# Scan layers of a four-layer network on one core: the step size's Softplus and its product with the input move two slots later, and GpSimd's share of B moves to other slots

## The chip, the cores and the metric

The kernel runs on one core of one Trainium2 chip. The core has five engines with their own instruction streams: PE (TensorE, matrix products), DVE (VectorE), ACT (ScalarE), POOL (GpSimd) and SP (SyncE, which here only issues DMA transfers). An engine executes its instructions strictly in the order in which the program lists them; engines wait for each other through semaphores. The metric is the device time in microseconds (us) of one execution.

## The reference

The network works on 8 images of 48 x 48 pixels and 96 channels. Four layers follow one another, each of the form x = x + layer(groupnorm(x)). Layers 0 and 3 are two-dimensional selective scans: a projection to 192 channels and a gate z, a 3 x 3 depthwise convolution with SiLU, four scans over the pixels (rows, columns, and both backwards), a layer norm, the gate and an output projection. Layer 1 is a pointwise network between an up- and a downsampling filter. Layer 2 has four selective scans along rows and columns. What matters here is the scan of layers 0 and 3 (K = 4 directions, 192 channels, 16 states, L = 2304 pixels):

```python
x_dbl = jnp.einsum('bkdl,kcd->bkcl', xs, x_proj_weight)
dts, Bs, Cs = jnp.split(x_dbl, [R, R + N], axis=2)
dts = jnp.einsum('bkrl,kdr->bkdl', dts, dt_projs_weight)
A = -jnp.exp(A_logs.astype(jnp.float32)).reshape(K, Din, N)
delta = jax.nn.softplus(dts + dt_projs_bias.reshape(K, Din)[None, :, :, None])

def step(h, inp):
    u, dl, Bv, Cv = inp
    dA = jnp.exp(dl[..., None] * A)
    h = h * dA + (dl * u)[..., None] * Bv[:, :, None, :]
    y = jnp.einsum('bkdn,bkn->bkd', h, Cv)
    return (h, y)
```

The step size delta is a Softplus; its product with the input u is the second thing that every scan needs. Each of the 192 x 16 pairs of channel and state is a recurrence of its own along the pixels.

## The kernel before

**Blocks, units, slots, turns.** `scans` (from L224) runs a scan layer. The work of one image and one direction is cut into five blocks of pixels (`BLKS`: four of 10 rows, 480 pixels, and one of 8 rows, 384 pixels, called a small block here). Layers 0 and 3 have 8 x 4 x 5 = 160 blocks each. A block has 24 units: a unit is 128 recurrences (32 channels by 4 states) along the block's pixels. Units are grouped in 8 slots of three (`ORDER`: slots 0 to 3 are the first half of the channels, 4 to 7 the second, the four state groups forwards and then backwards, so slots 3 and 4 share their states). Two slots make a turn; a block has four turns, called q0 to q3 here.

**What happens to a unit.** ACT computes dA = exp(A * delta) into PSUM (`make_da`, L329; two units are a pair, three pairs are a turn; the PSUM tile `ps_da` has two buffers, so ACT is at most two pairs ahead). A product du * B is made into the tile `dbu` (`make_dbu`, L305): for some units on DVE, which reads B from a copy in PSUM (`ps_b`, one buffer, written by ACT in `copy_b`, L286), and for the others on POOL, which reads B from the loaded tile `bc`. The tables `ON_POOL_SS` (layers 0 and 3) and `ON_POOL_L2` (layer 2) say how many of a slot's three units POOL makes; where it makes all three, no copy is made. `copy_b` has a case in which slot 4 reuses the copy of slot 3; it needs slot 3 to have one. DVE then runs the recurrence over a pair in place (`scan`, L337). POOL multiplies by C (`make_hc`, L343), and PE sums over the states (`reduce`, L359 to L365) into the tile `ps_y`; ACT copies the finished half block out (`done`, L762).

**The order.** It is written out by hand in the loop at the end of `scans`. For the turn t it lists: scan of pair 0; POOL's multiplication for the second slot of the turn before; DVE's product for slot 2t+2; exponentials of pair 1; POOL's units of slots 2t+2 and 2t+3; scan of pair 1; exponentials of pair 2; the copy of B for slot 2t+3 and DVE's product for it; `aside(2t)`; `begin` (boundary columns two turns ahead, POOL's L314 and L317); POOL's multiplication for the first slot; exponentials of the next turn's pair 0; scan of pair 2; the copy of B for slot 2t+4; `aside(2t+1)`. So products are made one turn before the scan that uses them.

**`aside`, the slot's side work.** Each call first lets ACT read what the guest put into PSUM in the slot before (`guest.settle`); then issues loads on SP (`LOAD_BC`: B and C of the next block at slots 1, 1, 6, 7, L270; `LOAD_DD_SS`: step sizes and products of the next block, in two halves at slots 3 and 5, L258, each 1452 KB when broadcast to 128 partitions); then advances the layer's own side work by one step (`side`: layer norm and output of the image before, group norm and convolution of the image after; the convolution ends in a SiLU group, L595 and L597, in slot 2 of ten of an image's twenty blocks); then runs the preparation steps that are due (`run`); and then lets the guest go on. The guest is layer 1, woven into the scans of layer 0 and layer 2. It matters in layer 0; layer 3 has none.

**Preparation of a block** (`stage1` of `ss2d`, L704 to L748). A block's steps are listed by slot, counted from the start of the second block before it; slots from 8 (`NG`) on lie in the block just before it:

- slot -1 and 1: projection to B, C and the low-rank step size (`s0`, L721, and its copy `s1`, L726)
- slot 3: store of B and C to DRAM (L729) and the first half of the step size's projection (L711)
- slots 4 and 5: the two halves with their bias into the tile `dds`, which has one buffer (`make_room`, `biased`, L715)
- slot 6: `s6`, the Softplus over both halves in one instruction (L739). The profile shows one `ACT_TABLE_LOAD` before it and one before the exponentials after it; the group is called the Softplus burst here
- slot 7: `make_du` (L507 to L515), POOL's product of step size and u, and two small memsets
- slots 8 and 9, that is slots 0 and 1 of the next block: `store_dd`, three stores to DRAM for each half (L492)

After them come the loads of slots 3 and 5 that bring both halves back, broadcast over partitions.

Of the kernel before, what the change touches and what calls it, by code (L numbers as in the profile page):

```python
# [29 lines left out]
NG = 8  # L30
# [14 lines left out]
FAR = 1e30  # L45
CH = 96

ON_POOL_SS = {2: 1, 3: 3, 5: 1, 6: 1, 7: 3}
ON_POOL_L2 = {4: 3, 6: 3, 7: 3}


# [51 lines left out]
def vss_stack_kernel(ctx: ExitStack, tc: tile.TileContext, i: dict, out: bass.AP):  # L103
# [386 lines left out]
    def store_dd(b, half):  # L490
        for g in range(3):
            nc.sync.dma_start(b.dd[half][:, 2 * g * b.m:2 * (g + 1) * b.m],  # L492
                              b.dds[32 * g:32 * g + 32, half].rearrange("p t m -> p (t m)"))

    def sizes(b, half):

        return [b.dds[:, half, n, b.at] for n in range(2)]

    def make_room(b, pools):
        b.room = pools["dds"].tile([DH, LEAD + 4 * WMAX], F32, tag="dds", name="dds")  # L500
        b.dds = b.room[:, LEAD:LEAD + 4 * b.m].rearrange("p (h t m) -> p h t m", h=2, t=2)

    def make_du(b, u):


        dt, du = [b.dds[:, :, n, b.at].rearrange("p h (r s) -> p h r s", s=SEG) for n in range(2)]
        nc.gpsimd.tensor_mul(du, dt, u)  # L507
        if b.m == b.n:
            at = SEG - 1 if b.rev else 0
            nc.gpsimd.memset(dt[:, :, :, at:at + 1], FAR)  # L510
        else:

            far = b.dds[:, :, :, b.came:] if b.back else b.room[:, :4 * b.m].rearrange("p (u m) -> p u m", m=b.m)[:, :, :LEAD + 1]
            nc.gpsimd.memset(b.dds[:, :, :, 0:1] if b.back else b.dds[:, :, :, b.goes:], 0.0)
            nc.gpsimd.memset(far, FAR)  # L515


    def ss2d(l, xin, xout, guest=None):
# [185 lines left out]
        def stage1(b):  # L704
            n = b.n
            u, uall = b.view(us[b.job], dirs[b.k][0]), b.view(uss[b.job], dirs[b.k][0])
            got = {}

            def raw(half):
                got["p"] = ps("s1", 1)  # L710
                nc.tensor.matmul(got["p"][:, :n], lhsT=wide("dtw", (2 * b.k + half) * DH), rhs=b.bcl[:, :n],  # L711
                                 start=True, stop=True)

            def biased(half):
                nc.scalar.activation(sizes(b, half)[0], got["p"][:DH, :n], AF.Identity,  # L715
                                     bias=w[f"{l}_dtb"][:, b.k, half:half + 1])

            def s0():
                got["p"] = ps("s1", 1)
                for half in range(2):  # L720
                    nc.tensor.matmul(got["p"][:, :n], lhsT=wide("xp", (2 * b.k + half) * NBC), rhs=uall[:, half],  # L721
                                     start=(half == 0), stop=(half == 1))

            def s1():
                b.bcl = pools["bcl"]
                nc.scalar.copy(b.bcl[:NBC, :n], got["p"][:NBC, :n])  # L726

            def s3():
                nc.sync.dma_start(b.bcd, b.bcl[:2 * NS, :n])  # L729
                raw(0)  # L730

            def s4():
                make_room(b, pools)
                biased(0)
                raw(1)

            def s6():
                both = b.dds[:, :, 0, b.at]
                nc.scalar.activation(both, both, AF.Softplus)  # L739

            def du():
                make_du(b, u)

            def store(half):
                return lambda: store_dd(b, half)

            return {-1: s0, 1: s1, 3: s3, 4: s4, 5: lambda: biased(1), 6: s6, 7: du,
                    NG: store(0), NG + 1: store(1)}  # L748

        def so_far(b, half):  # L750
            if b.job not in yss:
# [19 lines left out]
        for _ in conv(0, BLKS[:1]):  # L771
            pass
        scans(dirs, (0, 1, 3, 2), False, ON_POOL_SS, a, pools, ps, stage1, opening, done, side, tail, conv(0, BLKS[1:3]), guest)
        for _ in post(nb - 1, BLKS[:1]):
            pass
# [581 lines left out]
```

## Time and profile before

| | us |
|---|---|
| median of 3 executions | 17072.15 |
| their lowest and highest | 17067.16, 17077.52 |
| the profiled execution's own time | 17055.76 |
| its span, first to last instruction | 17054.0 |
| DVE busy | 15779.9 (93%) |
| POOL busy | 15177.8 (89%) |
| ACT busy | 13897.9 (81%) |
| PE busy | 13001.0 (76%) |

The span holds the three scan layers one after another: layer 0 until about 5740 us, layer 2 from about 5830 to 11550 us, layer 3 from about 11650 us on. A line of a group reads: line of the kernel, engine, operation, written tile <- read tiles, shapes, count, then busy us and mean ns of one instruction, and last the engine's idle time just before these instructions with what ended most of it. A line of a timeline reads: start us, duration us, engine, line, operation, tiles and shapes, count of merged instructions, and in brackets the idle time before it and what ended that. Durations in a timeline overlap the next instruction's start by some 0.05 to 0.1 us, so lengths in sums are taken from start to start. A line of stretches reads: from:to, length, then busy us and instruction counts of PE, PEld, DVE, ACT and POOL, the granted PE clock, the DMA engines' busy share and GB/s.

### The profile page before, as it was taken

The page shows a single profiled execution, that of the slowest core. Times are in us where ns is not written, and L with a number is a line of the kernel's source. Part 1 is how long each engine was busy: PE and PEld are TensorE (multiplying, and loading weights), DVE is VectorE, ACT ScalarE, POOL GpSimd, SP SyncE. Part 2 cuts the span into 40 slices and gives each one's busy share as a digit, 9 for nine tenths or more (in the row PEclk, how much of TensorE's full clock was granted, in tenths as well). Part 3 has the DMA queues.
Part 4 walks back from the last instruction along what each step waited for, and adds up shares of the span by engine and source line. Part 5 has one row for each costly group of instructions (what it writes and reads, how often), then busy time and mean ns, then how long its engine had stood idle before and what let it go on. Part 6 is the DMA issues. An engine that isn't in the chain of part 4 may idle for free.

```text
span 17054.0 us, 172343 instructions
## 1 busy us (share of the span) xinstructions
PE 13001.0 (76%) x53740; PEld 4650.8 (27%) x53740; DVE 15779.9 (93%) x9680; ACT 13897.9 (81%) x20972; POOL 15177.8 (89%) x7999
## 2 busy tenths in 40 slices
PE   6778787888787777777777777776777777777776
PEld 1223232333332333233323332221222222222221
DVE  7999999998999799999999999997999999999998
ACT  6888888888787688888888888886877878878876
POOL 7998998998889788888888888887999999999998
PEclk7888888888898899899989998887888878878887
DMA  4555555464555444544454444444555455555554
GB/s 148 180 173 169 180 168 186 166 187 165 175 173 177 137 156 164 163 159 163 157 170 158 158 163 158 161 156 133 176 175 175 175 172 178 176 169 178 176 175 143
DMA packets 931144, 2844.04 MB, mean 167 GB/s; under 512 B 396668, under 2 KB 464988, under 8 KB 803406
## 3 DMA queue, kind: packets, MB, share of 16 engines
q1 hardware_dynamic: 930222, 2833.03, 49.6%
q8 instruction: 422, 6.91, 0.2%
q14 instruction: 500, 4.10, 0.1%
HBM read 2384.40 MB, written 448.17 MB: 166 GB/s over the span
## 4 chain that ended last, share of the span: by engine, by line
POOL 24%; DVE 22%; ACT 21%; issue 18%; PE 10%; DMA 3%; SPq 1%; POOLq 0%; DVEq 0%; ACTq 0%
DVE dbu L337 14%; POOL dbu L343 14%; ACT ps_da L329 8%; POOL dbu L305 6%; DVE dbu L305 6%; ACT L329 3%; POOL dds L507 3%; PE ps_y L363 2%; ACT ps_b L286 2%; DMA dd<-dds 1%; DMA bc<-bcd 1%; PE ps_side L582 1%; ACT L926 1%; PE ps_s L711 1%; ACT zb L926 1%
## 5 line engine op out<-in xcount | busy, mean ns | idle before, releaser
L337 DVE TENSOR_TENSOR_SCAN dbu<-ps_da,dbu 128x968 f32<-128x968 f32 (+3 forms) x5760 | 11825.5, 2075 | 827.6 <-ACT ps_da L329 686.8
L343 POOL TENSOR_TENSOR dbu<-dbu,bc 128x1440 f32<-128x1440 f32 (+1 forms) x3840 | 10062.4, 2633 | 1531.0 <-DVE dbu L337 998.1
L329 ACT ACTIVATE ps_da<-dd,w_l_a 128x484 f32<-128x484 f32 (+3 forms) x11520 | 7420.1, 649 | 2411.1 <-DVE dbu L337 2183.4
L363 PE MATMUL ps_y<-dbu,w_red 128*32 128x480 f32 (+1 forms) x23040 | 4267.1, 656 | 1720.6 <-POOL dbu L343 1658.4
L365 PE MATMUL ps_y<-dbu,w_red 128*32 128x480 f32 (+1 forms) x7680 | 4227.6, 656 | 0.0
L305 DVE TENSOR_TENSOR dbu<-dd,ps_b 128x962 f32<-128x962 f32 (+5 forms) x2720 | 3813.9, 1402 | 185.2 <-ACT ps_b L286 135.2
L305 POOL TENSOR_TENSOR dbu<-dd,bc 128x481 f32<-128x481 f32 (+3 forms) x2080 | 3881.4, 1882 | 0.0
L363 PEld LDWEIGHTS ps_y<-dbu,w_red 128*32 128x32 f32 x23040 | 709.0, 117 | 5153.9 <-POOL dbu L343 3665.4
L286 ACT COPY ps_b<-bc 128x482 f32<-128x482 f32 (+3 forms) x2720 | 1449.0, 533 | 117.7 <-DVE dbu L305 104.2
L582 PE MATMUL ps_side<-xpad,w_l_cw 128*128 128x480 f32 (+1 forms) x2880 | 1324.2, 598 | 46.9 <-ACT g_room L1183 16.6
L329 ACT ACT_TABLE_LOAD x993 | 1274.0, 1283 | 17.5
L711 PE MATMUL ps_s<-bcl,square 128*128 128x480 f32 (+1 forms) x1280 | 876.8, 776 | 233.6 <-ACT dds L715 81.0
L359 PE MATMUL ps_y<-big,eye 128*128 128x480 f32 (+1 forms) x960 | 741.4, 860 | 257.5 <-ACT big L762 253.0
L721 PE MATMUL ps_s<-big,square 128*128 128x480 f32 (+1 forms) x1280 | 848.6, 794 | 66.7 <-ACT g_room L1183 18.3
L507 POOL TENSOR_TENSOR dds<-dds,big 96x960 f32<-96x960 f32 (+1 forms) x320 | 706.2, 2207 | 118.3 <-ACT dds L739 115.6
L582 PEld LDWEIGHTS ps_side<-xpad,w_l_cw 128*128 128x128 f32 x2880 | 560.8, 205 | 792.9 <-issue 675.8
L874 PE MATMUL ps_sb<-xpad,square 128*128 128x480 f32 (+1 forms) x1280 | 608.0, 621 | 89.0 <-ACT g_room L1183 38.0
L365 PEld LDWEIGHTS ps_y<-dbu,w_red 128*32 128x32 f32 x7680 | 647.9, 117 | 0.0
L874 PE MATMUL ps_sa<-xpad,square 128*128 128x480 f32 (+1 forms) x1280 | 521.2, 548 | 0.0
L917 PE MATMUL ps_sa<-xpad,square 128*128 128x480 f32 (+1 forms) x320 | 255.6, 895 | 339.6 <-ACT g_room L1183 108.8
L762 ACT COPY big<-ps_y 96x480 f32<-96x480 f32 (+1 forms) x640 | 471.1, 736 | 38.2 <-PE ps_y L365 36.9
L711 PEld LDWEIGHTS ps_s<-bcl,square 128*128 128x128 f32 x1280 | 250.6, 241 | 762.6 <-ACT dds L715 327.7
(250 smaller groups left out, 12540.6 us busy)
## 6 DMA issues: line engine op xcount, KB each, us to landing
dd<-dd SPq DMA_DIRECT2D x512, 1452.0 KB
bc<-bcd SPq DMA_DIRECT2D x1536, 480.0 KB
dd<-dd SPq DMA_DIRECT2D x256, 1440.0 KB
dd<-dds SPq DMA_DIRECT2D x1536, 121.0 KB
dd<-dd SPq DMA_DIRECT2D x128, 1164.0 KB
bc<-bcd SPq DMA_DIRECT2D x384, 384.0 KB
dd<-dds SPq DMA_DIRECT2D x768, 120.0 KB
dd<-dd SPq DMA_DIRECT2D x64, 1152.0 KB
```

The costliest lines, as they stand in the source:

```text
L286: nc.scalar.copy(bps[t][:, :bcs[t][0].shape[1]], bcs[t][0])
L305: engine.tensor_mul(o, du, by.unsqueeze(1).to_broadcast([P, hi - lo, by.shape[1]]))
L329: nc.scalar.activation(da[:, at:at + b.m], b.got[half][:, u % 3, 0, :], AF.Exp, scale=a[:, b.k, ci:ci + 1])
L337: nc.vector.tensor_tensor_scan(db, da, db, 0.0, ALU.mult, ALU.add)
L343: nc.gpsimd.tensor_mul(h, h, bcs.pop(2 * t + sub)[1].unsqueeze(1).to_broadcast([P, 3, n]))
L363: nc.tensor.matmul(y[32 * g:32 * g + 32, :n], lhsT=wc["red"][:, :32], rhs=hc[:, g, b.at], start=False, stop=(slot == 3))
L365: nc.tensor.matmul(y[DH:, :n], lhsT=wc["red"][:, 32:], rhs=hc[:, 2, b.at], start=False, stop=(slot == 3))
L507: nc.gpsimd.tensor_mul(du, dt, u)
L582: nc.tensor.matmul(pu[:, :n], lhsT=flat[:, at:at + P], rhs=xpad[:, r0 + dy:r0 + dy + nr, dx:dx + W], start=(tap == 0), stop=(tap == 8))
L711: nc.tensor.matmul(got["p"][:, :n], lhsT=wide("dtw", (2 * b.k + half) * DH), rhs=b.bcl[:, :n], start=True, stop=True)
L721: nc.tensor.matmul(got["p"][:, :n], lhsT=wide("xp", (2 * b.k + half) * NBC), rhs=uall[:, half], start=(half == 0), stop=(half == 1))
L874: nc.tensor.matmul(got["u", half][:, :n], lhsT=wide("cw", at), rhs=shifted(off), start=(tap == 0), stop=(tap == 3))
```

## The change

Three edits, for layers 0 and 3 alone; layer 2 is not touched.

- The Softplus moves from slot 6 of the second block before to slot 8, that is from q3 of that block to q0 of the next one (slot 0).
- POOL's product and memsets move from slot 7 to slot 9 (slot 1 of the block before), and all six stores follow them there; before, three stores stood in slot 8 and three in slot 9.
- POOL makes all three units of slot 1 and one of slot 3, where it made one of slot 2 and three of slot 3. Its total stays 9 of 24. Slot 3 now has a copy of B, so `copy_b` lets slot 4 reuse it, and slot 1 has none.

```diff
-ON_POOL_SS = {2: 1, 3: 3, 5: 1, 6: 1, 7: 3}
+ON_POOL_SS = {1: 3, 3: 1, 5: 1, 6: 1, 7: 3}
...
             def du():
                 make_du(b, u)
-
-            def store(half):
-                return lambda: store_dd(b, half)
-
-            return {-1: s0, 1: s1, 3: s3, 4: s4, 5: lambda: biased(1), 6: s6, 7: du,
-                    NG: store(0), NG + 1: store(1)}
+                for half in range(2):
+                    store_dd(b, half)
+
+            return {-1: s0, 1: s1, 3: s3, 4: s4, 5: lambda: biased(1), NG: s6, NG + 1: du}
```

## The prediction

> **What bounds the kernel.** I read the page's busy shares and groups first, then busy time by stretches, then the list of waits, then the timelines of single blocks.
>
> ```profile
> PE 13001.0 (76%) x53740; PEld 4650.8 (27%) x53740; DVE 15779.9 (93%) x9680; ACT 13897.9 (81%) x20972; POOL 15177.8 (89%) x7999
> ...
> L337 DVE TENSOR_TENSOR_SCAN dbu<-ps_da,dbu 128x968 f32<-128x968 f32 (+3 forms) x5760 | 11825.5, 2075 | 827.6 <-ACT ps_da L329 686.8
> ...
> 2000.00:3000.00 1000.00, 810.40 (x3639) 326.59 (x3639) 924.88 (x560) 838.11 (x1302) 897.61 (x510) 0.87 0.56 177
> ...
> 13000.00:14000.00 1000.00, 740.49 (x2868) 224.72 (x2872) 970.01 (x604) 788.54 (x1199) 949.63 (x539) 0.80 0.51 173
> ```
>
> The stretches list PE, PEld, DVE, ACT, POOL. DVE is the bound: layer 0 (60 to 5700 us) leaves it about 75 us idle in 1000, layer 3 (from 11640 us) only 30. Most of that idle time is a scan waiting for its exponentials from ACT: the list of waits has 642 of them, the longest 4.2 us. So only DVE's gaps can move: layer 0 and layer 3 hold some 590 us of them.
>
> A block is four turns, q0 to q3, of two slots. In each, DVE runs scan, product (even slot), scan, product (odd slot), scan. ACT runs one block of layer 3 so (start, duration):
>
> ```profile
> 12742.76 1.28 ACT L595 ACT_TABLE_LOAD   x1
> ...
> 12745.19 1.28 ACT L329 ACT_TABLE_LOAD   x1
> ...
> 12758.91 0.56 ACT L286 COPY ps_b<-bc 128x482 f32<-128x482 f32 x1
> 12759.49 1.28 ACT L739 ACT_TABLE_LOAD   x1
> 12760.78 1.01 ACT L739 ACTIVATE dds<-dds 96x960 f32<-96x960 f32 x1
> 12761.81 1.28 ACT L329 ACT_TABLE_LOAD   x1
> ```
>
> and DVE beside it:
>
> ```profile
> 12740.51 1.63 DVE L305 TENSOR_TENSOR dbu<-dd,ps_b 128x1443 f32<-128x1443 f32 x1
> ...
> 12744.14 1.13 DVE L305 TENSOR_TENSOR dbu<-dd,ps_b 128x962 f32<-128x962 f32 x1
> ...
> 12747.89 2.17 DVE L337 TENSOR_TENSOR_SCAN dbu<-ps_da,dbu 128x968 f32<-128x968 f32 x1 [0.53 <-ACT ps_da L329]
> ...
> 12760.87 1.63 DVE L305 TENSOR_TENSOR dbu<-dd,ps_b 128x1443 f32<-128x1443 f32 x1
> 12762.42 4.26 DVE L337 TENSOR_TENSOR_SCAN dbu<-ps_da,dbu 128x968 f32<-128x968 f32 x2
> ```
>
> Two bursts, two geometries. After the Softplus burst (the three lines from 12759.49) the first exponential starts at 12763.10: 3.61 us. It sits in q3, where DVE has two products of three units (1.55 us each, start to start), and the next scan just does not wait. The Silu burst (12742.76 to the exponential at 12746.49, 3.73 us) sits in q1, with products of three and two units (1.55 and 1.05): there the scan waits 0.53.
>
> **Part 1: the burst goes to q0, and q0 gets q1's geometry.** The units change makes slots 2 and 3 products of three and two units on DVE. With T0 the start of slot 2's product: copy of B ends T0+2.17 (product 1.55, then the copy starts 0.12 late and takes 0.50), burst +3.61, two exponentials and signal 1.45, so T0+7.23. DVE arrives at T0+1.55+2.08+1.05+2.08 = 6.76. Stall 0.47 per full block, close to Silu's 0.53; by the same steps 1.2 in a block of 8 rows (scans 1.69, products 1.25 and 0.85). Going through the DVE and ACT timelines block by block, with the side work that stands at q0 (DVE side work of 0.5 us or more covers the stall; an ACT reading for the guest or a normalization lengthens it): layer 0 has 72 bare full blocks (34 us), 17 with ACT work before the burst (15), 40 covered (0), 31 small (48): 97 us. Layer 3: 93 bare (43), 35 covered (0), 30 small (41): 84 us. Added: 181 us (155 and 205 if a bare block costs 0.41, Silu's wait less the shorter burst, or 0.53).
>
> What goes is the wait of scans 2 to 8.5 us after the burst's first load. Summed over the timeline: 150 us in layer 0, 33 in layer 3. It is large in layer 0 because the guest's products of slot 5 are read by ACT just ahead of the burst. They stay in q3, which DVE now passes faster (no slot 1 product): exponentials must be ready at T0+5.71. Taking each block's measured end of that reading, 25 blocks of layer 0 still wait, 20 us (bounds 0 and 40). Removed: 183-20 = 163. **Net +18 us.**
>
> **Part 2: units.** GpSimd does 9 of 24 units before and after, DVE 15, with the same shapes, so both busy times stay. Slot 4 now reuses slot 3's copy of B: one ACT copy (0.55) less in 319 blocks, 175 us of ACT. I cost it at nothing: it lies in q0 and q3 where ACT waits for DVE anyway; were that not so, it would be worth at most those 175. DVE's turns become 8.8, 8.8, 7.3, 7.8 us instead of 7.3, 8.8, 7.3, 9.4. Hence three small things:
> - Side work of DVE in slot 1 waits for PE. DVE comes there 1.55 later, so each wait shrinks by up to that: 27 us in layer 0, 15 in layer 3: **-42** (bounds -58, all of those waits, and 0, if PE slips as much).
> - Side work in slot 7 (39 operations fed by PE) comes 1.55 earlier, while GpSimd, by the row sums, enters q3 0.9 us less late: 0.65 each, **+25** (bounds 0 and 60).
> - In small blocks a product waits for the boundary copy L317 behind GpSimd's units of slots 2 and 3 (18 us); GpSimd now has one unit there, 1.03 us, not 3.74: **-18** (bounds -18 and +18, should the three units in q3 delay other boundary copies as much).
>
> **Part 3: product and stores to slot 1.** GpSimd: one product (1.88, or 2.70 when columns are read) and memsets of 0.1, moved past two multiplications by C (2.7 each) and slot 3's unit. Summing q0 from its entry 2.1 us late: 2.7+1.0+2.7+2.1 ends 10.6 us after q0's start (11.3 for columns); the next multiplication was due at 9.3, so GpSimd is 1 to 2 us late, and its next consumer, slot 5's unit, has 4 us in hand: 0. On SP, the six stores (0.42 each) now stand behind the two B/C loads of slot 1 and wait for the product:
>
> ```profile
> 12769.21 1.55 SPq L492 DMA_DIRECT2D dd<-dds  x3
> 12770.93 0.52 SPq L258 DMA_DIRECT2D dd<-dd  x1
> ```
>
> Queued behind them are slot 1's and 2's guest transfers, the load L258 of slot 3 and the store of B and C. The first three stores are issued at 12766.66 now, as soon as the product is done. The load issues 6.4 us into q0 and is wanted 26 us into it. Then: product 11, stores 2.8, first landing: 15.5, wanted at 28 (small block 14.8 and 23). By the stretches of 1 us, the traffic of such a load, issued at 13033.2, ends at 13039.5: 6.3 us. So it is hidden, with 6 and 2 us over. The next block's step sizes (L715, slot 4) reuse the buffer, at 21.8 against stores landed by 16.5: 0. At each layer's start slot 1's copy and DVE product (2.28 us, ahead of the first exponential) go: **-5** (bounds -5 and +8, two steps of later stores).
>
> **Sum:** 18-42+25-18-5 = -22 us on the profiled execution's 17055.76 us (span 17054.0): 17034. The median shown is 17072.15, 16.4 above, so **17050 us**, -0.13%. About 0.2%, 34 us, is what tells a change of this kernel from none.
>
> ACT's table loads, by the rows above: an instruction follows a load's end within 0.03 us. The Trainium skill ("ScalarE: Activation LUTs", What ACT_TABLE_LOAD costs) adds a drain of some 1.38 us to each switch; by it a burst would stall every uncovered q0 2.8 us more, about +670 over the 243 turns left uncovered. The trace disagrees, and I go by it.
>
> **Rivals.**
> - *A load comes late (slower).* For it: 2 us of margin in small blocks, two 1452 KB loads back to back, one SP queue. Against: 20 us of margin now, and no scan or product waits for that load after the starts. If both halves land together, 2.9 MB at the 400 GB/s of those stretches, with 1.3 us until bytes flow, takes 8.6 us, past the 8.2 there; each us beyond costs 61 us over the 61 small blocks. It decides from 10 us: two late us are +122 on the sum: 17170. Milder, one: 17110.
> - *Even turns drain other gaps (clearly faster).* In layer 0 scans wait 165 us in the rest of the block, most for exponentials that came late behind guest readings; layer 3 has 73. If the lighter q3 and the missing copy take a third, 80 us: 16970. Against: most of these lie in q1 and q2, which the change leaves as they are.
> - *Only the stall moves.* 181 us come, 183 go, PE-fed waits cancel too: 17070.
>
> **How the numbers follow.** Sum as worked out 0.48 (own range 17010 to 17090, from the bounds of parts 1 and 2, so 0.14 of it is faster by over 0.2%), late load 0.19, drained gaps 0.20, stall only moved 0.13 (of which 0.05 slips to slower by ACT's lateness). Faster 0.34, same 0.42, slower 0.24. The range reaches to the drained gaps and to a load late by one: 16965 to 17120.
>
> **What would show it.** In layer 3's bare blocks, a scan's wait of 0.4 to 0.5 us after each Softplus, at the second turn's start, where now there is none; in layer 0's convolution blocks the wait after Softplus down from 1.3 to about 0.6 us a block; ACT copies of L286 fewer by some 319; DVE and GpSimd busy times unchanged. Wrong if a product L305 waits for dd's load, if SP waits on the product long after slot 3, or if GpSimd's multiplications, not DVE, set layer 3's pace.

## The result, and the profile after

The changed kernel takes 17140.79 us (median of 5, 17132.05 to 17144.43), the kernel before 17067.16 beside it: 1.0043 times as long, 95% interval 1.0032 to 1.0054. The forecast was 17050 us, range 16965 to 17120. It is slower by some 74 us, where a small gain was expected.

The profiled executions differ by 88.6 us. First scan to last scan:

| | before | after | difference | forecast, its terms added by layer |
|---|---|---|---|---|
| layer 0 | 5642.2 | 5729.0 | +86.8 | about -55 |
| layer 2 (not touched) | 5707.9 | 5712.8 | +4.9 | 0 |
| layer 3 | 5363.7 | 5366.1 | +2.4 | about +35 |

So nearly all of the loss lies in layer 0, although layers 0 and 3 got the same edits. (The differences of a few us elsewhere are the size of what two executions differ by: layer 2, which no run edits, takes 5704 to 5714 us in the profiled runs.) The busy shares and the scans' group on the page of the changed kernel, and its stretches (columns as before: PE, PEld, DVE, ACT, POOL):

```profile
PE 12967.6 (76%) x53740; PEld 4655.0 (27%) x53740; DVE 15789.2 (92%) x9680; ACT 13766.5 (80%) x20653; POOL 15193.3 (89%) x7999
...
L337 DVE TENSOR_TENSOR_SCAN dbu<-ps_da,dbu 128x968 f32<-128x968 f32 (+3 forms) x5760 | 11837.3, 2076 | 948.3 <-ACT ps_da L329 790.5
```

```profile
2000.00:3000.00 1000.00, 802.12 (x3526) 318.07 (x3526) 898.60 (x543) 804.29 (x1242) 876.28 (x499) 0.86 0.56 172
13000.00:14000.00 1000.00, 726.05 (x2908) 226.29 (x2912) 973.31 (x597) 780.04 (x1171) 952.97 (x532) 0.83 0.53 177
```

DVE and POOL do the same work; what grew is the scans' wait for exponentials, 686.8 to 790.5 us. The stretch in layer 0 lost 26 us of DVE work in 1000, the one in layer 3 gained 3. ACT did 131 us less, and no gain of it can be seen.

Layer 3 behaves as the prediction drew it. One of its blocks, ACT and then DVE (lines from about L745 on have numbers two lower than before):

```profile
12821.46 0.56 ACT L286 COPY ps_b<-bc 128x482 f32<-128x482 f32 x1 [0.18 <-DVE dbu L305]
12822.04 1.28 ACT L739 ACT_TABLE_LOAD   x1
12823.34 1.01 ACT L739 ACTIVATE dds<-dds 96x960 f32<-96x960 f32 x1
12824.36 1.28 ACT L329 ACT_TABLE_LOAD   x1
12825.66 1.37 ACT L329 ACTIVATE ps_da<-dd,w_l_a 128x484 f32<-128x484 f32 x2
```

```profile
12819.80 1.63 DVE L305 TENSOR_TENSOR dbu<-dd,ps_b 128x1443 f32<-128x1443 f32 x1
...
12823.43 1.13 DVE L305 TENSOR_TENSOR dbu<-dd,ps_b 128x962 f32<-128x962 f32 x1
12824.47 2.17 DVE L337 TENSOR_TENSOR_SCAN dbu<-ps_da,dbu 128x968 f32<-128x968 f32 x1
12827.06 2.17 DVE L337 TENSOR_TENSOR_SCAN dbu<-ps_da,dbu 128x968 f32<-128x968 f32 x1 [0.42 <-ACT ps_da L329]
```

With T0 = 12819.80 the scan starts at T0+7.26 (forecast T0+7.23) and waits 0.42 (forecast 0.47). On SP the stores wait for POOL's product, and the load of the next step sizes goes right behind them:

```profile
12829.33 2.65 SPq L492 DMA_DIRECT2D dd<-dds  x6
12832.30 0.52 SPq L258 DMA_DIRECT2D dd<-dd  x1
```

No scan waits for that load in either layer, and a product only once (2.08 us at 5485.57 us, in layer 0).

Where layer 0's time went is seen by adding up DVE's idle time in its timeline by place in the block (a turn has scans 1 to 3; "product" is L305):

| DVE idle, us | layer 0 before | layer 0 after | layer 3 before | layer 3 after |
|---|---|---|---|---|
| q0, scan 1 (after the burst in slot 6, before) | 148.5 | 9.7 | 33.0 | 0 |
| q0, product of slot 2 | 0 | 16.1 | 0 | 0 |
| q0, scan 2 | 18.6 | 73.5 | under 6 | under 6 |
| q1, scan 1 (after the burst in slot 0, after) | 8.2 | 166.6 | 0 | 76.9 |
| side work in slot 1 that waits for PE | 43.2 | 13.7 | 14.6 | 1.3 |
| q1, product of slot 4 (boundary copy L317) | 5.0 | 0 | 13.1 | 0 |

Two entries were not forecast: the second scan of a block, and how large the burst's stall is in layer 0. Behind both stands the same thing. Here is one and the same block of layer 0 in both kernels, at the same point of layer 1's work. First ACT and DVE of the kernel before:

```profile
3982.50 1.28 ACT L739 ACT_TABLE_LOAD   x1
...
3986.12 1.37 ACT L329 ACTIVATE ps_da<-dd,w_l_a 128x484 f32<-128x484 f32 x2
3987.42 0.54 ACT L286 COPY ps_b<-bc 128x482 f32<-128x482 f32 x1
3988.29 0.40 ACT L1194 COPY g_room<-ps_s 73x288 f32<-73x288 f32 x1 [0.33 <-PE ps_s L1192]
3988.59 2.65 ACT L329 ACTIVATE ps_da<-dd,w_l_a 128x484 f32<-128x484 f32 x4
```

```profile
3987.52 2.17 DVE L337 TENSOR_TENSOR_SCAN dbu<-ps_da,dbu 128x968 f32<-128x968 f32 x1 [2.19 <-ACT ps_da L329]
3989.61 1.13 DVE L305 TENSOR_TENSOR dbu<-dd,ps_b 128x962 f32<-128x962 f32 x1
3990.66 2.17 DVE L337 TENSOR_TENSOR_SCAN dbu<-ps_da,dbu 128x968 f32<-128x968 f32 x1
```

Then the changed kernel, PE first:

```profile
4042.58 0.48 PE L365 MATMUL ps_y<-dbu,w_red 128*32 128x384 f32 x1
4043.00 1.88 PE L582 MATMUL ps_side<-xpad,w_l_cw 128*128 128x480 f32 x4
4044.71 2.14 PE L1190 MATMUL ps_s<-g_w2q,g_room 128*128 128x96 f32 x18
```

```profile
4042.06 0.54 ACT L286 COPY ps_b<-bc 128x482 f32<-128x482 f32 x1
4046.89 0.40 ACT L1192 COPY g_room<-ps_s 73x288 f32<-73x288 f32 x1 [4.29 <-PE ps_s L1190]
4047.19 2.65 ACT L329 ACTIVATE ps_da<-dd,w_l_a 128x484 f32<-128x484 f32 x4
4049.78 0.55 ACT L286 COPY ps_b<-bc 128x482 f32<-128x482 f32 x1
4050.34 1.28 ACT L739 ACT_TABLE_LOAD   x1
```

```profile
4044.34 1.63 DVE L305 TENSOR_TENSOR dbu<-dd,ps_b 128x1443 f32<-128x1443 f32 x1
4048.59 2.17 DVE L337 TENSOR_TENSOR_SCAN dbu<-ps_da,dbu 128x968 f32<-128x968 f32 x1 [2.61 <-ACT ps_da L329]
...
4055.35 2.17 DVE L337 TENSOR_TENSOR_SCAN dbu<-ps_da,dbu 128x968 f32<-128x968 f32 x1 [1.46 <-ACT ps_da L329]
```

Before, DVE waits 2.19 us for the burst, and the guest's reading (L1194), which stands on ACT ahead of the block's second pair of exponentials, waits only 0.33 for its products and is over before DVE wants that pair. After, the burst is gone from there and DVE arrives at once: the block's first scan starts 7.2 us after the first scan of q3 (4042.28 after 4035.13), where it was 11.7 (3987.52 after 3975.78). PE's products come about where they came: 18 of them, behind the sums over states and four convolution products, end 11.7 us after that scan of q3, 12.5 before. So ACT now stands 4.29 us at the reading, with the exponentials behind it. DVE pays 2.61 us at the second scan, and since the third pair, the copy of B and the burst are pushed back with it, 1.46 us more after the burst: 4.07 in place of 2.19.

### The profile page after: what moved, and what is told of

Read it like the earlier page. It is cut to its first block, busy times and chain, and to the rows that moved or that the text cites. A ratio compares the mean times of both kernels' runs of the same rounds, so it can differ in the third digit from the quotient of the medians.

```text
span 17142.6 us, 171368 instructions
## 1 busy us (share of the span) xinstructions
PE 12967.6 (76%) x53740; PEld 4655.0 (27%) x53740; DVE 15789.2 (92%) x9680; ACT 13766.5 (80%) x20653; POOL 15193.3 (89%) x7999
## 4 chain that ended last, share of the span: by engine, by line
ACT 28%; DVE 28%; issue 18%; PE 13%; POOL 10%; DMA 3%; SPq 0%; DVEq 0%; POOLq 0%; ACTq 0%
DVE dbu L337 18%; ACT ps_da L329 10%; DVE dbu L305 8%; POOL dbu L343 6%; ACT L329 5%; POOL dbu L305 3%; PE ps_y L363 3%; ACT ps_b L286 2%; ACT L739 2%; PE ps_side L582 1%; ACT dds L739 1%; POOL dds L507 1%; ACT L924 1%; PE ps_s L711 1%; PE ps_y L359 1%
## 5 line engine op out<-in xcount | busy, mean ns | idle before, releaser
L337 DVE TENSOR_TENSOR_SCAN dbu<-ps_da,dbu 128x968 f32<-128x968 f32 (+3 forms) x5760 | 11837.3, 2076 | 948.3 <-ACT ps_da L329 790.5
L363 PE MATMUL ps_y<-dbu,w_red 128*32 128x480 f32 (+1 forms) x23040 | 4214.6, 653 | 1334.7 <-POOL dbu L343 1328.6
L365 PE MATMUL ps_y<-dbu,w_red 128*32 128x480 f32 (+1 forms) x7680 | 4176.2, 653 | 0.0
L305 DVE TENSOR_TENSOR dbu<-dd,ps_b 128x962 f32<-128x962 f32 (+5 forms) x2720 | 3813.5, 1402 | 183.3 <-ACT ps_b L286 149.5
L305 POOL TENSOR_TENSOR dbu<-dd,bc 128x481 f32<-128x481 f32 (+3 forms) x2080 | 3898.1, 1884 | 41.7 <-DMA dd<-dd 25.1
L363 PEld LDWEIGHTS ps_y<-dbu,w_red 128*32 128x32 f32 x23040 | 728.1, 118 | 4745.8 <-POOL dbu L343 3121.2
L286 ACT COPY ps_b<-bc 128x482 f32<-128x482 f32 (+3 forms) x2400 | 1282.0, 534 | 153.0 <-DVE dbu L305 100.1
L329 ACT ACT_TABLE_LOAD x996 | 1277.9, 1283 | 17.5
L365 PEld LDWEIGHTS ps_y<-dbu,w_red 128*32 128x32 f32 x7680 | 665.1, 118 | 0.0
L760 ACT COPY big<-ps_y 96x480 f32<-96x480 f32 (+1 forms) x640 | 471.7, 737 | 21.5 <-PE ps_y L365 21.2
```

The source lines that it names most:

```text
L286: nc.scalar.copy(bps[t][:, :bcs[t][0].shape[1]], bcs[t][0])
L305: engine.tensor_mul(o, du, by.unsqueeze(1).to_broadcast([P, hi - lo, by.shape[1]]))
L329: nc.scalar.activation(da[:, at:at + b.m], b.got[half][:, u % 3, 0, :], AF.Exp, scale=a[:, b.k, ci:ci + 1])
L337: nc.vector.tensor_tensor_scan(db, da, db, 0.0, ALU.mult, ALU.add)
L363: nc.tensor.matmul(y[32 * g:32 * g + 32, :n], lhsT=wc["red"][:, :32], rhs=hc[:, g, b.at], start=False, stop=(slot == 3))
L365: nc.tensor.matmul(y[DH:, :n], lhsT=wc["red"][:, 32:], rhs=hc[:, 2, b.at], start=False, stop=(slot == 3))
```

## The experiments

Lengths of layer 0 are first scan to last scan; waits are added up by place as in the table. "Readings" are the instructions by which ACT takes the guest's products (layer 1's) out of PSUM. Kernels that leave out a part of the guest's work ran once each.

**The two halves alone.** The table of units alone, on the kernel before:

```diff
-ON_POOL_SS = {2: 1, 3: 3, 5: 1, 6: 1, 7: 3}
+ON_POOL_SS = {1: 3, 3: 1, 5: 1, 6: 1, 7: 3}
```

> Before with the new table of GpSimd's units alone; the burst stays in slot 6, product and stores in slots 7 and on. The last quarter of a block then has one DVE product less (1.55 us) under the same burst, so by the working of the prediction each first scan that is not covered waits 1.55 us more: some 240 turns over both layers, 250 to 400 us, 17310 to 17470 us in all. Theory G (the guest's late PSUM readings on ScalarE, standing ahead of the second exponentials of a block, hid under a longer last quarter before): DVE enters the block late here because it waits for the burst, so the readings stay hidden and the second scan of layer 0's blocks waits about what it did before, 10 to 35 us in all. Rival U (the table itself, with three of GpSimd's units in the last quarter, makes the second scan late): 50 to 75 us there, as in the changed kernel (73.5).

17287.0 us, 1.0132 (1.0115 to 1.0149): 23 us under the expected range. The first scans wait 290.8 us in layer 0 and 132.7 in layer 3. The second scans of layer 0 wait 7.7 us, so the table by itself does not make them late; rival U falls. And the burst with product and stores alone (the changed kernel with the old table):

```diff
-ON_POOL_SS = {1: 3, 3: 1, 5: 1, 6: 1, 7: 3}
+ON_POOL_SS = {2: 1, 3: 3, 5: 1, 6: 1, 7: 3}
```

> The changed kernel with the old table of units: burst in slot 0, product and stores in slot 1, GpSimd's units in slots 2 and 3. DVE then has only the two units of slot 2 (1.05 us) in the first quarter; ScalarE has one copy of B less ahead of the burst, so it comes 1.25 us late in a bare block instead of 0.47. Layer 3: 180 to 200 us of wait at the second quarter's first scan against 33 us at the first quarter's before; layer 0: 160 to 230 against 148. In all 150 to 300 us slower than before, 17220 to 17370 us. Theory G: the last quarter has its product back and no burst, so the second scan of layer 0's blocks waits at most 20 us in all. Rival B (the burst's new place makes the second scan late): 50 us or more there.

17372.16 us, 1.0182 (1.0166 to 1.0197), just over the range. The scan after the burst waits 255.1 us in layer 0, more than the 160 to 230 expected, and 173.9 in layer 3, less than the 180 to 200. The second scans of layer 0 wait 47.5: neither at most 20 (G) nor 50 and more (B). Here q3 has its second product back, and they still wait. So the longer q3 alone did not hide the readings, as G had it; the wait for the burst at the first scan did so too: without that wait the second scans go from 18.6 to 47.5 us, and the shorter q3 on top of it takes them to 73.5. The first two scans of a block together wait 167 us in layer 0 before, 298 with the table alone, 51 with the burst alone, 83 with both.

**The guest taken out of layer 0.** The PSUM work of layer 1 is left out of layer 0 and done between layers 0 and 2, in both kernels alike (line 764 or 766, and the end of `ss2d`):

```diff
-            guest.banks = lambda slot, clear: (["side"] if clear else []) + (["s1"] if slot in (2, 5, 6) else [])
+            guest.banks = lambda slot, clear: []
...
             guest.avail = nb
+            guest.banks = lambda slot, clear: ["side", "s1"]
+            while guest.made < 6:
+                guest.settle()
+                guest.turn(2, True)
+            guest.settle()
```

> The changed kernel with layer 1's PSUM work taken out of layer 0; it is done by itself between layers 0 and 2, so the whole time says nothing and only layer 0, first to last scan, is read. Theory G: layer 0 behaves like layer 3. Second scans wait less than 20 us in all (73.5 in the changed kernel), the scan after the burst 75 to 105 us (166.6), and the layer's length is within -15 and +30 us of the same cut of the kernel before (with the guest it was +86.7; layer 3, which has none, +2.5). Rival S (layer 0's own side work or the loads, not the guest): the difference stays 60 to 100 us.

> The kernel before with layer 1's PSUM work taken out of layer 0 and done by itself after it, as control for the same cut of the changed kernel. Theory G: the first scan's wait after the burst falls from 148 us to 30 to 60 us, as in layer 3 (33), and layer 0 is 100 to 300 us shorter than 5640 us, within 30 us of the changed kernel's. Rival S: layer 0's first scans still wait 100 us or more, and the layer is 60 to 100 us shorter than the changed kernel's.

Layer 0 takes 5366.5 us with the change and 5366.9 without it: the difference is gone, -0.4 where it was +86.8. With the change second scans wait 2.8 us and the scan after the burst 77.1; without it the first scans wait 33.0. These are layer 3's numbers (76.9 and 33.0). Rival S falls: without the guest, the loads, the stores, the convolution and layer 0's own side work cost nothing new. DVE's list of waits over layer 0, before and then after, both without the guest:

```profile
DVE dbu L337 <- ACT ps_da L329: 78.8, 104, 3.4
```

```profile
DVE dbu L337 <- ACT ps_da L329: 110.5, 173, 4.4
```

and with it, before and after:

```profile
DVE dbu L337 <- ACT ps_da L329: 267.4, 246, 4.2
```

```profile
DVE dbu L337 <- ACT ps_da L329: 339.4, 306, 4.4
```

(The part of a wait that the trace puts down to other releasers is not in these lines; it is in the sums by place.)

**One pair of exponentials ahead of one reading.** The change alone, nothing left out; in q3 of layer 0's blocks the second pair of the next block is listed ahead of `aside(7)`, in which the guest's products of slot 6 are read:

```diff
-            make_da(t, 1)
+            if (t, 1) not in das:
+                make_da(t, 1)
...
             copy_b(at + 4)
+            if q == NG // 2 - 1 and guest and not restart:
+                make_da(t + 1, 1)
             finish(at + 1)
             aside(at + 1)
```

> The changed kernel, in layer 0 alone, with a block's second pair of exponentials put ahead of the side work of the slot before (slot 7), so that ScalarE runs them before the guest's reading of a product that TensorE got in slot 6. Nothing is left out. Theory G2 (that reading, waiting for TensorE, is what the second scan waits for): the waits of the second scan and of the product behind it fall in layer 0 from 90 us (73.5 and 16.1) to 10 to 35; the scan after the burst keeps 130 to 180 us, since the reading still stands ahead of the burst; layer 0 is 40 to 90 us shorter than 5729 us and the kernel 17050 to 17105 us. Rival L (ScalarE is simply late by the guest's sum of work, in whatever order): the wait moves to the next scans and the kernel stays within 15 us of 17141.

17104.18 us, 1.0025 of before (1.0016 to 1.0034), 37 us less than the changed kernel; layer 0 5685.3, 43.7 less. The second scans' 73.5 us are gone to nothing. The products of slots 2 and 3 wait 31.5 us: 10.3 at slot 2's, where late loads of B cost 16.1 in the changed kernel (see the rivals below), and 21.2 at slot 3's, where nothing waited and whose copy of B now stands behind the reading. The scan after the burst keeps 171.3. All within G2, the time just. So the order on ACT makes the second scans late, and rival L, by which the sum of the guest's work would make ACT late anyhow, falls. The reordering wins back half of layer 0's 86.8 us; the other half stays, with the reading still ahead of the burst. DVE in layer 0 of this kernel:

```profile
DVE dbu L337 <- ACT ps_da L329: 278.2, 264, 4.9
...
DVE dbu L305 <- ACT ps_b L286: 31.5, 26, 2.9
```

**Which products.** The guest is kept out of slot 6 of the shared bank, with the change and without; or out of slot 5, with it. What layer 1 then lacks is done after layer 0 by the loop shown above. For slot 6:

```diff
-(["s1"] if slot in (2, 5, 6) else [])
+(["s1"] if slot in (2, 5) else [])
```

For slot 5 the tuple is `(2, 6)`.

> The changed kernel with layer 1's products in layer 0 kept out of slot 6 of the bank that the slots share (slots 2 and 5 stay); what is missing of layer 1 is done by itself after layer 0, so only layer 0 is read. Theory G2: no reading stands between the first and second exponentials of a block: second scan and product wait 5 to 30 us in all (90 in the changed kernel), the scan after the burst 85 to 130 (166.6; 77 without any guest). Rival L: both fall only by the guest's share that is gone, about a third of what the guest adds: 60 or more, and 135 or more.

> As the cut without slot 6, but slot 5 is left out and slots 2 and 6 stay: as many of layer 1's products are missing from layer 0. Theory G2: the readings of slot 6's products still stand ahead of the second exponentials: second scan and product wait 55 to 100 us in all, the scan after the burst 125 to 170. Rival L: the same as without slot 6, within 15 us on each of the two.

> Control for the cut without slot 6: the kernel before with layer 1's products in layer 0 kept out of slot 6 of the shared bank, the missing part of layer 1 done by itself after layer 0; only layer 0 is read. The changed kernel with the same cut took 5576 us there. Theory G2 (the change costs layer 0 its time through the readings of slot 6's products): the kernel before takes 5560 to 5625 us with this cut, so that the change costs 15 us at most, where with slot 6 it costs 87. Rival (the guest's sum of work, not these readings): it takes 5480 to 5550 us, and the change still costs 30 to 90.

| us, layer 0 | length | second scan + product of slot 2 | scan after the burst |
|---|---|---|---|
| changed | 5729.0 | 73.5 + 16.1 | 166.6 |
| changed, without slot 6 | 5576.4 | 17.4 + 9.1 | 121.8 |
| changed, without slot 5 | 5633.2 | 37.2 + 13.1 | 170.7 |
| before | 5642.2 | 18.6 + 0 | 148.5 |
| before, without slot 6 | 5577.0 | 7.7 + 0 | 136.8 |

Without slot 6's products the change costs layer 0 nothing: 5576.4 against 5577.0. The cut of slot 5 leaves twice as much at the second scan and 49 us more after the burst; its 50.3 us lie a little under what G2 expected, its 170.7 just over, but both are too far from the cut of slot 6 for L. Two limits: the kernel before was not run without slot 5, so what the change costs there is not known; and leaving products out takes work from PE as well as readings from ACT. Only the reordering above separates the two, for the second scan; no run puts the burst of the changed kernel ahead of a reading. What ACT stands waiting at such readings in layer 0, before and then after, is on its list of waits (`ps_s` is the shared bank, `ps_side` the side bank):

```profile
ACT g_room L1194 <- PE ps_side L1192: 64.8, 41, 3.4
ACT g_room L1194 <- PE ps_s L1192: 46.3, 33, 5.5
ACT g_room L1183 <- PE ps_side L1181: 38.4, 37, 3.3
...
ACT g_room L1183 <- PE ps_s L1181: 7.8, 11, 1.4
```

```profile
ACT g_room L1192 <- PE ps_s L1190: 97.4, 47, 5.9
ACT g_room L1192 <- PE ps_side L1190: 83.0, 40, 4.8
ACT g_room L1181 <- PE ps_s L1179: 58.3, 36, 3.8
ACT g_room L1181 <- PE ps_side L1179: 46.8, 45, 3.1
```

The two rows of `ps_s` grow from 54 to 156 us. Of the 73.5 us of second scans in the changed kernel, 67 have a reading as ACT's longest wait ahead of them, of the shared bank or the side bank.

**The size of the burst's stall.** The prediction reckons it as DVE's way past the burst against ACT's. In the changed kernel GpSimd's unit of slot 3 is moved to slot 6, so that q0 has two products of three units:

```diff
-ON_POOL_SS = {1: 3, 3: 1, 5: 1, 6: 1, 7: 3}
+ON_POOL_SS = {1: 3, 5: 1, 6: 2, 7: 3}
```

> The changed kernel with GpSimd's unit of slot 3 moved to slot 6: DVE's first quarter, which carries the Softplus burst, has two products of three units, as the last quarter had before. If the burst's stall is DVE's way past it against ScalarE's, as the prediction reckons it (T0+7.23 against T0+7.26 now instead of 6.76): in layer 3 the scan after the burst waits 20 to 40 us in all instead of 76.9, what is left being the small blocks. In layer 0 the readings of the guest still make ScalarE late: 90 to 135 us instead of 166.6, and second scan and product still wait 60 to 110 (90). Kernel 17050 to 17125 us. Rival (the stall belongs to the burst, its table loads and what it waits for, whatever DVE does): 65 us or more in layer 3, and no gain.

In layer 3 the wait after the burst falls from 76.9 to 30.4 us: 34.6 to 0.9 in full blocks, 42.3 to 29.5 in the small ones. In layer 0 it falls from 166.6 to 112.8, and second scan and product keep 86.0. These waits are as reckoned. The time, 17125.29 us (1.0038 of before, 1.0026 to 1.0051), is just over the range: layer 0 is as long as it was (5729.5), since the 54 us come back at other waits, most of all at the scans of q3 (first scans there 48.5 to 60.7, second 53.7 to 74.5). In 67 of these 74.5 us ACT's longest wait ahead of the scan is a reading of the side bank.

**Two candidates, and what order can do before the change.** The same reckoning on the kernel before says that its convolution burst in q1 needs two products of three units, too:

```diff
-ON_POOL_SS = {2: 1, 3: 3, 5: 1, 6: 1, 7: 3}
+ON_POOL_SS = {2: 1, 3: 3, 6: 2, 7: 3}
```

> A candidate: the kernel before with one more of GpSimd's units in slot 6 and none in slot 5, so that the second quarter, which carries the convolution's burst, has two products of three units like the last quarter. If ScalarE's burst alone sets that wait: the third quarter's first scan waits 0 to 15 us instead of 53 in each of layers 0 and 3, and the kernel is 20 to 90 us faster, 16975 to 17045 us. Rival (GpSimd comes 1 us later out of the third quarter, and its units, its multiplications or the guest's readings behind them come late): the waits of the fourth and first quarter grow by 60 us or more in layer 0, and the kernel is within 20 us of before or slower.

17030.5 us, 0.9981 (0.9972 to 0.9990): faster than both kernels. The first scan of q2 waits 21.9 us instead of 53.7 in layer 0, 21.4 instead of 53.2 in layer 3 (full blocks wait 1 us in all, the small ones 21, so it is above the expected 15). Layer 3 keeps 21.5 us of it; layer 0, where 3.4 us are left, gave it back at other scans. The rival falls: in layer 0 the scans of q3 wait 23 us more and those of q0 no more, not 60, and the kernel is 32 us faster.

To that, the Softplus ahead of the guest's reading in slot 6:

```diff
-            return {-1: s0, 1: s1, 3: s3, 4: s4, 5: lambda: biased(1), 6: s6, 7: du,
+            return {-1: s0, 1: s1, 3: s3, 4: s4, 5: lambda: biased(1), 5.5: s6, 7: du,
...
             nblk, slot = at // NG + 1, at % NG
+            run(at - 0.5)
             if guest:
                 guest.settle()
```

(The loop ahead of the first block gets `run(t - 0.5)` likewise.)

> The candidate with one of GpSimd's units moved from slot 5 to slot 6 (17030 us; Softplus in slot 6 as in the kernel before), with the Softplus put ahead of the guest's reading in slot 6 instead of behind it. Theory G: of the 148.6 us that layer 0's first scans wait there, the 33 of layer 3 are the burst and the other 115 are ScalarE standing at a reading that waits for TensorE with the burst behind it; with the burst run in that time the wait falls to 40 to 90 us, second scans grow to 15 to 40, layer 0 is 40 to 100 us shorter than 5639, and the kernel 16935 to 16995 us. Rival (the reading comes later than the burst's end, so the order does not matter): 110 us or more, within 15 us of 17030.

17016.77 us, 0.9975 (0.9965 to 0.9985): the fastest kernel of the study. But the first scans still wait 122.9 us, over the 110 at which the rival wins, and the time misses G's range. The rival's reason is not what the trace shows, though. With the burst put ahead, ACT hardly stands at a reading any more: of the first scans' waits, those that have a reading and idle time of ACT ahead of the exponentials fall from 41.5 us in the candidate to 6.5. What stays is mostly 92.6 us (82.3 in the candidate) in which a reading lies ahead of the exponentials and ACT is busy throughout, with the burst and the reading itself (0.3 to 1.2 us). So G took 115 us for standing where some 40 were, and the order could win back only that part: 26 us. The scans' group, in which 583.3 of 782.2 us are ACT's:

```profile
L337 DVE TENSOR_TENSOR_SCAN dbu<-ps_da,dbu 128x968 f32<-128x968 f32 (+3 forms) x5760 | 11818.1, 2074 | 782.2 <-ACT ps_da L329 583.3 <-issue 95.0 <-POOL dbu L317 33.1
```

And in layer 0 the next block's first pair ahead of that reading as well:

```diff
             run(at - 0.5)
+            if slot == NG - 2 and guest and not restart:
+                make_da(at // 2 + 1, 0)
             if guest:
                 guest.settle()
...
-            make_da(t + 1, 0)
+            if (t + 1, 0) not in das:
+                make_da(t + 1, 0)
```

> As the one with the burst ahead of the reading, and in layer 0 the next block's first pair of exponentials also ahead of it. Theory G: the first scan waits 25 to 50 us in layer 0 (33 in layer 3), but the copy of B for slot 2 and the second pair now stand behind the reading: 20 to 60 us on the second scan and the product ahead of it. Layer 0 50 to 120 us shorter than 5639 us, kernel 16915 to 16985 us. Rival (what ScalarE gives up at one scan it owes at the next): the sum of the two scans' waits is as in the other kernel of this order, within 15 us, and so is the time.

17078.98 us, 1.0009 (1.0000 to 1.0019). First and second scan wait 78.1 + 61.0 = 139 us, against 122.9 + 20.4 = 143: as the rival said, what ACT gives up at one scan it owes at the next; G misses with the first scan, and with the time. The time did not stay, either; it is 62 us longer. 52 of these are new idle time of DVE in layer 0, and much of it is side work that waits for PE (the copy of the variance, L631, 25.5 us against 9.4; the normalization, L652, 25.6 against 9.3). That the later readings keep PSUM banks from PE would fit; no run here shows it.

## Why the prediction was wrong

The measured terms beside those of the prediction:

| step | forecast, us | measured, us |
|---|---|---|
| burst's stall in layer 3 | +84 | +76.9 |
| burst's stall in layer 0 | +97 | +158.4 |
| first scans' wait removed, layer 3 | -33 | -33.0 |
| first scans' wait removed, layer 0 | -150 + 20 | -148.5 + 9.7 |
| second scans, layer 0 | no term | +54.9 |
| product of slot 2, layer 0 | no term | +16.1 |
| side work in slot 1 | -42 | -42.8 |
| side work in slot 7 | +25 | about +10 |
| boundary copy L317 | -18 | -18.1 |
| layer starts | -5 | -6.1 |
| 319 copies less on ACT | 0 | nothing seen |

**Right.** The geometry of the burst holds: in layer 3 the stall is 0.42 us in most full blocks that have one (forecast 0.47), about 1.2 in a small one. Where a unit of half a microsecond is moved to DVE's stretch beside a burst, the stall goes from the full blocks and shrinks by 0.4 in the small ones, in two runs. So the terms of layer 3, and those of slot 1, of the boundary copies and of the starts, came out nearly to the number. ScalarE's table loads cost what the rows said: 1.28 us each, with 0.02 us behind them at 12824.36. The Trainium skill ("ScalarE: Activation LUTs", What ACT_TABLE_LOAD costs) gives the same 1283 ns for a load but adds a drain of some 1380 ns to every switch. By an estimate from that page, two drains would make layer 3's stall 3.2 us where it is 0.42, so the trace still disagrees. One slip in the sum itself: with 165 bare full blocks, 0.41 or 0.53 instead of 0.47 us moves the 181 us by 10, not to 155 or 205.

**The step that failed** is in part 1, in two places. "They stay in q3, which DVE now passes faster" followed only the readings of slot 5's products to the first scan (9.7 us remain there, inside the bounds of 0 and 40). The readings of slot 6's products come one slot later, between the block's first and second pair of exponentials; before, the wait at the first scan covered them, and that cover was taken for a stall to be removed. It got no term: +54.9 at the second scan. And "17 with ACT work before the burst" was counted in the old timeline, where those readings were over before DVE came. In the changed kernel 101 of layer 0's 159 bursts that can be placed in the trace have one or more readings or other side work ahead of the block's second pair; their blocks stall 1.34 us each after the burst (135 us), and the 57 with none on the way to the burst 0.52 us each (30 us). Take away what those 101 stall more, 83 us, and layer 0 is left with 75, close to the 77 of layer 3 and of layer 0 without the guest. Together the two places, with the 16 us of the next paragraph, are 132 us too little, against 111 between the forecast of -22 and the profile's +88.6; the leftover in q3, slot 7 and layer 3's stall, which were forecast too high, make up for some 32, and of the 10 or so that then remain 5 are layer 2's. That these three errors run the other way is luck.

**The rivals.** "A load comes late" named the right sign and the wrong load: the loads of step sizes are late for DVE once, by the 2.08 us above. A load of B is late more often, for 16.1 us of waits at the product of slot 2: in eight blocks of layer 0 ACT's copy waits 3.4 to 5.2 us for it, and in six of them it stands on SP behind the guest's two stores L1158. Before, the copies in these blocks waited 1.5 us at most for the same loads, and the product never, since in seven of the eight the first scan was held for 0.35 to 1.63 us. "Even turns drain other gaps" failed: the scans' waits in the rest of layer 0's blocks are 170 us before and 173 after (q3's second scan grew from 44.3 to 53.7, others shrank). "Only the stall moves" is right for layer 3 (+2.4 us) and for layer 0 without the guest (-0.4). The rival that came true, readings that lose their cover, was not on the list.

**What stays open.** Why layer 0 gives back what is won at one place (54 us in the run with two products of three units in q0, 28 of 32 at q2 in the faster candidate) was not followed to one cause; the runs show where it reappears, most of all at the scans of q3 behind readings of the side bank, not which engine sets that pace.

## What to carry to other kernels

A stall can be the cover of something else: before you count a wait as removed, list what the other engines do during it, above all in-order work behind a wait of its own, and ask when the next consumer will then arrive. Where a part of the program has extra work woven in (here a guest layer), cost the change on that part by itself, since the same edit was worth +2.4 us without it and +86.8 with it. A fixed burst on another engine is hidden best beside the stretch with the most work on the bounding engine: moving one unit of half a microsecond there made layer 3 11.8 and 21.5 us shorter, in two runs, while layer 0, with the guest, kept nothing and 3.4 us.

## Not expected of the hardware

Issuing two DMA transfers held the queue of SP for long. The guest's pair of stores L1158 (288 and 40.5 KB) takes 3.1 to 8.1 us on SP in the changed kernel, 6.6 us or more in eight of its 32 times; before (L1160) it is 3.2 to 8.0, and 6.4 or more in eight. Meanwhile nothing behind it is issued. From 1105 to 1120 us of the example, 4752 of 5053 packets are under 512 bytes; whether that is the reason, no run shows. In the changed kernel, SP and then ACT:

```profile
1109.54 7.24 SPq L1158 DMA_DIRECT2D upd<-g_room  x2
1116.82 2.64 SPq L270 DMA_DIRECT2D bc<-bcd  x4
```

```profile
1121.30 0.48 ACT L286 COPY ps_b<-bc 128x386 f32<-128x386 f32 x1 [3.65 <-DMA bc<-bcd]
```
